# Selective-scan layers: a second buffer of turned x, one evacuation per projection, y summed in four column quarters, scatters spaced

## The chip, the core and the metric

The kernel runs on one NeuronCore of a Trainium2 chip. Its time is the device time of one execution in microseconds; where several runs are shown, the median is taken. The engines are TensorE (PE, with its weight loads as PEld), VectorE (DVE), ScalarE (ACT), GpSimd (POOL) and SyncE (SP, which issues most DMAs). Each engine takes its instructions in the order of the program, and engines wait for one another through semaphores.

## The reference, cut to what matters

An image batch of 4 x 64 x 64 positions with 96 channels passes through four layers. The first two are selective-scan layers, and the change lies in them alone. Cut to its core, one of them is:

```python
xz = x @ in_proj_w.T;  xc, z = split(xz)              # 192 channels each
xc = silu(depthwise_conv3x3(xc) + conv_b)
xs = stack([xc[order_k] for k in range(4)])           # four directions over the 4096 positions
x_dbl = einsum("bkdl,kcd->bkcl", xs, x_proj)          # dt (rank 6), B (16), C (16)
delta = softplus(dt_proj(dts) + dt_bias)
h = h * exp(delta * A) + (delta * u) * B              # step by step over 4096 positions
y = sum_n h[n] * C[n]                                 # 16 states
out = layernorm(merge of the 4 directions + D * xs) * silu(z) @ out_proj
```

In the first layer the four orders are two diagonal snakes and two radial orders, and the directions are merged with position-dependent weights. In the second they are rows, columns and both of them backwards, and they are added. A feed-forward part of layer 1 and the layers 2 and 3 (linear attention, a Fourier mixer, two small networks with fp8 products) follow. The change leaves them as they are.

## The kernel before

`scan_layers` works off eight batches: four images of the first layer (L0, `ordered`), then four of the second (L1). A batch has 4 directions (`kd`) x 4 segments of 1024 positions. A segment has 24 groups, each of 32 channels x 4 states on 128 partitions: 6 channel blocks (`cb`) x 4 state groups (`sg`). For a group

- ACT computes `da` = exp(dt * A) (`decay`, L1072), up to four groups ahead of the scan;
- DVE multiplies `t` = u * B (`enter`, L1076) and scans `h` = da * h + t (`recur`, L1083). DVE's order is fixed: two products, then the two scans;
- ACT keeps the last state (`keep`, L1094), POOL multiplies `hc` = h * C (`leave`, L1098);
- PE sums `hc` over the states into `y` in PSUM (`collect`, L1107).

At each of the six channel blocks PE first spreads `u` over 128 partitions (`spread_u`, L1065, "spread 0" to "spread 5" below): the product of groups 0, 4, 8, 12, 16 and 20 waits for it. When two blocks (8 groups) are summed, ACT copies `y` out (`yc`, L1136), PE turns it (L1148, "turn") and ACT writes it into `rows` (L1152). At the end of a segment `rows` goes to `y_tok` in DRAM: in L0's directions 0 and 1 as eight indirect scatters issued by POOL (L1162), else by SP.

While a segment is scanned, the next one is prepared (`prepare`). Its x is fetched position by position into `x_got`; PE turns it (`turn_x`, L897) and ACT copies it into `xs` (L908, L913); PE projects it in four parts (`project`, L934); ACT evacuates each part (`split`, L947 to L953); ACT forms the parts of softplus (`low`, L991 to L995, and `log`, L1006, between two table loads, since the rest of ACT needs another table); PE adds its four terms with identity matmuls (L1014, "sums") and ACT copies out `dt` (`keep_dt`, L1017); POOL multiplies `dtu` = dt * xs (L1023). `dt`, B and C go through DRAM to be spread over partitions. All of these use the one PSUM bank `m`, as does the turn of `y`. `xs` has one buffer, so the turning of the next x waits for the last `dtu` product of the segment before.

The order of the instructions in a batch is written by a planner, `Flow`: each operation has an estimated occupancy, a latency to other engines, a due time, and a mark `hard` for those that DVE waits for. It simulates the queues and emits the operations in that order. Where it sees PE idle it calls `keep_busy` (L1125), which issues matmuls with zero weights into the open sum, so that the PE clock stays up. Between batches a second planner, `Plan`, runs the merge of the batch that ended (`merge`) side by side with the convolution of the batch after the next (`front`); their tiles (`z_rows`, `xc`, `y_rows`, `yt`, `dx`, `halo`) lie in the pool `tmp` and are used only there. These stretches are called transitions below.

## Time and profile before

| | us |
|---|---|
| median of 3 runs (15260.49 to 15279.87) | 15266.5 |
| profiled execution, its own time | 15402.95 |
| its span | 15401.2 |
| start to the first product of the first batch | 386.2 |
| eight batches, first product to the end of the last scan: 1349.9, 1331.0, 1337.2, 1325.4 (L0), 1302.1, 1293.6, 1301.2, 1294.5 (L1) | 10534.9 |
| seven transitions between them: 211.9, 212.8, 225.4, 209.1, 159.7, 155.8, 98.7 | 1273.4 |
| after the last scan (last merge, layer 1's feed-forward, layers 2 and 3) | 3206.7 |

The four stretches are read from the first and last DVE instruction of each batch (lines 1076 and 1083) and add up to the span. Over the whole span PE is busy 90%, DVE 83%, POOL 60%, ACT 54%, the 16 DMA engines about a third; but PE's share holds the zero-weight matmuls, and the shares mix batches, transitions and the later layers. In a batch DVE has the most to do, and what is looked for is the time in which it stands still there.

### The profile page before, as it was taken

What the parts mean: (1) busy time and instruction counts of PE and PEld (TensorE: products, weight loads), DVE (VectorE), ACT (ScalarE), POOL (GpSimd) and SP (SyncE); (2) the same over time, 40 slices, a digit from 0 to 9 for tenths busy, and PEclk for the clock granted to TensorE, in tenths of its full rate; (3) what the DMA queues carried; (4) which work ended last, traced back from release to release, by engine and by line L of the source; (5) the groups of instructions that cost most, each with busy time, mean ns of one, the idle gap of its engine ahead of it and who ended that gap; (6) DMA issues with size and microseconds to landing.
All of it is one profiled execution on the core that took longest, in us unless ns stands there. A gap on an engine that the chain in (4) does not pass through costs nothing. (4 is left out here: it accounts for less than half of the span.)

```text
span 15401.2 us, 196660 instructions
## 1 busy us (share of the span) xinstructions
PE 13827.4 (90%) x74369; PEld 5096.1 (33%) x74369; DVE 12827.4 (83%) x9642; ACT 8327.7 (54%) x13421; POOL 9203.3 (60%) x4657
## 2 busy tenths in 40 slices
PE   8899899989998999899989998999899789998877
PEld 3233333333333333333333333333233244443344
DVE  1999799978997899799979997999899856555655
ACT  3666466646664666466656665666566423232333
POOL 0788678867886688667747774777577620000123
PEclk9999899989998999899989999999999999998888
DMA  2333433343334333433343334333433400000122
GB/s 67 117 113 125 150 111 111 126 148 112 111 127 146 106 118 128 148 116 117 123 152 124 118 124 152 126 118 120 156 119 120 142 10 11 19 15 12 52 72 71
DMA packets 662768, 1637.49 MB, mean 106 GB/s; under 512 B 102822, under 2 KB 268460, under 8 KB 658045
## 3 DMA queue, kind: packets, MB, share of 16 engines
q1 hardware_dynamic: 624956, 1549.37, 31.4%
q0 software_dynamic: 36864, 75.55, 1.7%
q8 instruction: 588, 9.63, 0.3%
q14 instruction: 360, 2.94, 0.1%
HBM read 1295.03 MB, written 329.58 MB: 105 GB/s over the span
## 5 line engine op out<-in xcount | busy, mean ns | idle before, releaser
L1098 POOL TENSOR_TENSOR hc<-h,bc 128x1024 f32<-128x1024 f32 x3072 | 7198.4, 2365 | 2216.1 <-DVE h L1083 1909.0
L1083 DVE TENSOR_TENSOR_SCAN h<-da,state,t 128x1024 f32<-128x1024 f32 x2304 | 5300.4, 2355 | 26.0 <-ACT state L1094 16.3
L1072 ACT ACTIVATE da<-dts,L_A_logs 128x1024 f32<-128x1024 f32 x3072 | 3520.0, 1151 | 1832.2 <-DVE h L1083 1786.7
L1076 DVE TENSOR_TENSOR t<-u,bc 128x1024 f32<-128x1024 f32 x3072 | 3629.8, 1239 | 267.6 <-PE u L1065 193.5
L1107 PE MATMUL y<-hc,gather_y 128*32 128x512 f32 x12288 | 3529.1, 620 | 311.9 <-POOL hc L1098 241.7
L1125 PE MATMUL y<-L_diag,zeros 96*32 96x256 f32 x7824 | 1986.3, 386 | 0.0
L1083 DVE TENSOR_TENSOR_SCAN h<-da,t 128x1024 f32<-128x1024 f32 x768 | 1717.4, 2287 | 17.3 <-ACT da L1072 9.1
L1065 PE MATMUL u<-dtu,spread 32*128 32x512 f32 x3072 | 1573.1, 632 | 120.0 <-DVE t L1076 109.2
L1125 PEld LDWEIGHTS y<-L_diag,zeros 96*32 96x32 f32 x7824 | 852.8, 111 | 1425.0 <-issue 926.1
L1107 PEld LDWEIGHTS y<-hc,gather_y 128*32 128x32 f32 x12288 | 595.8, 109 | 2021.1 <-issue 1029.1
L934 PE MATMUL m<-xs,proj 96*128 96x512 f32 (+1 forms) x2048 | 1070.2, 641 | 67.3 <-ACT spare L1152 32.5
L1642 DVE SCALAR_TENSOR_TENSOR hcv<-padv,taps,hcv 128x2048 f32<-128x2048 f32 x384 | 902.2, 2350 | 13.4
L1566 POOL MEMSET padp<- 128x2448 f32 x32 | 68.6, 2143 | 1400.8 <-PE d L1606 1378.3
L1023 POOL TENSOR_TENSOR dtu<-dt,xs 96x1024 f32<-96x1024 f32 x256 | 603.0, 2356 | 506.1 <-ACT dt L1017 501.1
L1606 PE MATMUL d<-padp,diag 32*32 32x512 f32 x25600 | 885.7, 601 | 2.0 <-ACT hcp L1621 2.0
L1065 PEld LDWEIGHTS u<-dtu,spread 32*128 32x128 f32 x3072 | 521.4, 188 | 943.6 <-issue 588.0
L1017 ACT COPY dt<-m 96x512 f32<-96x512 f32 x512 | 297.2, 580 | 694.5 <-PE m L1014 690.0
L1014 PE MATMUL m<-dtu,ident 96*96 96x512 f32 x1024 | 563.8, 632 | 72.7 <-ACT dt L1017 65.9
L1606 PEld LDWEIGHTS d<-padp,diag 32*32 32x32 f32 x25600 | 484.4, 103 | 369.8 <-issue 196.9
L934 PEld LDWEIGHTS m<-xs,proj 96*128 96x128 f32 (+1 forms) x2048 | 324.6, 181 | 770.6 <-issue 483.8
L947 ACT ACTIVATE sp_z<-m,L_dtb 96x512 f32<-96x512 f32 x512 | 350.0, 684 | 409.5 <-PE m L934 393.5
L1014 PE MATMUL m<-sp_log,ident 96*96 96x512 f32 x1024 | 539.2, 608 | 0.0
(275 smaller groups left out, 15495.8 us busy)
## 6 DMA issues: line engine op xcount, KB each, us to landing
bc<-bc_dram SPq DMA_DIRECT2D x1024, 512.0 KB
dts<-dt_dram SPq DMA_DIRECT2D x768, 512.0 KB
dt_dram<-dt SPq DMA_DIRECT2D x256, 384.0 KB
y_tok<-spare SPq DMA_DIRECT2D x64, 768.0 KB
dt<-y_tok SPq DMA_DIRECT2D x128, 384.0 KB
x_tok<-y_rows SPq DMA_DIRECT2D x32, 768.0 KB
z_t<-z_rows SPq DMA_DIRECT2D x64, 384.0 KB
dx<-x_tok SPq DMA_DIRECT2D x64, 384.0 KB
```

The source lines that it names most:

```text
L934: nc.tensor.matmul(v.ps, seg.proj[:, src, to], seg.xs[:, src, chunks[j]], start=src == 0, stop=src == 1)
L1014: nc.tensor.matmul(v.ps, k.ident[:C, :C], term[:, half, chunks[j]], start=at == 0, stop=at == 3)
L1023: nc.gpsimd.tensor_mul(seg.dtu[:, half], v.dt[:, half], seg.xs[:, half])
L1065: self.nc.tensor.matmul(seg.u[:, cols], self.spread[rows, :], seg.dtu[rows, half, cols], start=True, stop=True)
L1072: self.nc.scalar.activation(gr.da, gr.seg.dts[gr.cb], AF.Exp, scale=scale)
L1076: self.nc.vector.tensor_mul(gr.t, gr.seg.u, self.bc[:, 0, gr.sg, :])
L1083: self.nc.vector.tensor_tensor_scan(gr.h[:, order], gr.da[:, order], gr.t[:, order], start, op0=ALU.mult, op1=ALU.add)
L1098: self.nc.gpsimd.tensor_mul(gr.hc, gr.h, self.bc[:, 1, gr.sg, :])
L1107: nc.tensor.matmul(seg.y[at : at + GC, :], self.gather_y, gr.hc[:, part * CH : (part + 1) * CH], start=gr.sg == 0, stop=gr.sg == NSG - 1, ...
L1125: self.nc.tensor.matmul(gr.seg.y[at : at + GC, :256], self.zeros, gr.seg.bt.lay.diag.rearrange("p h t c -> p (h t c)")[:, :256], start=Fal ...
L1606: nc.tensor.matmul(pc[i][j * 32 : (j + 1) * 32, :], diag[mine, ON_PE.index(t), tap, :], pad[mine, j * 8 + dy : j * 8 + dy + 8, dx : dx + H ...
L1642: nc.vector.scalar_tensor_tensor(to, win, wt, to, op0=ALU.mult, op1=ALU.add)
```

## The change

1. **xs.** The tiles that only the transitions used become views of one tile `area` of 7 x 1024 values a partition, in the same number and size. Its last two sevenths (where `yt`, `dx` and `halo` lie) hold `xs` of the odd segments; the even ones keep their tile. The turning of x now waits for the `dtu` product of the segment before the last.
2. **Evacuation.** Each projected part leaves PSUM in one instruction (bias added, 128 rows with B and C, or 96). Abs and Relu follow from SBUF, as two more steps of `low` for each half. The projections no longer wait for the sums of the segment before; the first `low` step does.
3. **Sums of y.** `collect` issues four matmuls of 256 columns into four 32-column strips of the array in place of two of 512 into two. `turn` and `keep_rows` follow that layout (two copies in place of one), and so do the row order of `scan_idx` and the whole-segment stores (pieces of 384 values in place of 768).
4. **Scatters.** In the planner each scatter depends on the one before having landed.
5. **Planner.** `collect` counts 0.46 for 0.87; preparation is due 8 us later; a PE operation that waits for POOL is planned 1 us later; in front of hard operations `keep_busy` fills 0.35 of the gap for 0.7.

```diff
 class Op / Flow.run
+        self.lands = False
-                self.fill(start - free[engine])
+                self.fill(start - free[engine], 0.35 if op.hard else 0.7)
-                user.seen = max(user.seen, done if user.engine == engine else done + op.lat)
+                pad = 1.0 if (engine, user.engine) == ("POOL", "PE") else 0.0
+                near = user.engine == engine and not op.lands
+                user.seen = max(user.seen, done if near else done + op.lat + pad)
 Stream
+        self.area = k.t(w, [128, 7 * SEG], "area")
+    def shared(self, rings):
+        ...
+        cut("z_rows", 2, C, h=2, t=CH)
+        cut("xc", 3, 128, t=CH)
+        cut("y_rows", 1, 128, f=2, t=4, d=DI)
+        cut("yt", 1, C, h=2, t=CH)
+        cut("dx", 1, 128, t=CH // 128, d=DI)
+        cut("halo", 2, C, e=2, w=HW)
 prepare
-            x = Op(engine, occ, emit, deps, due=base + at, **kw)
+            x = Op(engine, occ, emit, deps, due=base + at + 8.0, **kw)
-                seg.xs = k.t(self.seg, [C, 2, SEG], "xs")
+                if seg.i % 2:
+                    seg.xs = self.area[:C, 5 * SEG :].rearrange("p (h t) -> p h t", h=2)
+                else:
+                    seg.xs = k.t(self.seg, [C, 2, SEG], "xs")
-                here += [b.get(("u", h)) for h in range(2)]
+                here += [before.before.o.get(("u", h)) for h in range(2)] if before and before.before else []
-            if what == 0:
-                nc.scalar.activation(v.z[:, half, cols], ps[:C], AF.Abs, bias=bias)
-            elif what == 1:
-                nc.scalar.activation(v.dt[:, half, cols], ps[:C], AF.Relu, bias=bias)
-            elif lay.bias_bc is None:
-                nc.scalar.copy(v.bc[:, cols], ps[C:])
+            if half == 0:
+                nc.scalar.activation(v.both[:, 0, cols], ps, AF.Identity, bias=lay.bias_bc[:, kd : kd + 1])
             else:
-                nc.scalar.activation(v.bc[:, cols], ps[C:], AF.Identity, bias=lay.bias_bc[C:, kd : kd + 1])
+                nc.scalar.activation(v.dt[:, 1, cols], ps, AF.Identity, bias=bias)
 low(half, what): Exp, 1 + z, 1 - r before; after:
+                nc.scalar.activation(z[:, half], dt[:, half], AF.Abs)
+                nc.scalar.activation(z[:, half], z[:, half], AF.Exp, scale=-1.0)
+                nc.scalar.activation(dt[:, half], dt[:, half], AF.Relu)
+                ...
 collect
-        for part in range(2):
-            at = (part * 2 + cb % 2) * GC
+        for part in range(4):
+            at = part * GC
             nc.tensor.matmul(
-                seg.y[at : at + GC, :],
+                seg.y[at : at + GC, cb % 2 * 256 : (cb % 2 + 1) * 256],
                 self.gather_y,
-                gr.hc[:, part * CH : (part + 1) * CH],
+                gr.hc[:, part * 256 : (part + 1) * 256],
 keep_busy
-        for _ in range(int((gap - 0.15) * 0.7 / 0.215)):
+        for _ in range(int((gap - 0.15) * share / 0.215)):
 turn, keep_rows
-        for j in range(CH // 128):
-            v = seg.ycs[pair][:, j::4] if fours else seg.ycs[pair][:, j * 128 : (j + 1) * 128]
-            nc.tensor.transpose(ps[:, j, :], v, k.ident)
+        for b in range(2):
+            mine = seg.ycs[pair][:, b * 256 : (b + 1) * 256]
+            for t in range(2):
+                nc.tensor.transpose(ps[:, b * 2 + t, :], mine[:, t::2] if twos else mine[:, t * 128 : (t + 1) * 128], k.ident)
-        self.nc.scalar.copy(seg.rows[:, :, :, pair * 64 : (pair + 1) * 64], ps)
+        for b in range(2):
+            at = pair * 64 + b * GC
+            self.nc.scalar.copy(seg.rows[:, :, :, at : at + GC], ps[:, b])
 store
-            return [Op("POOL", 1.25, partial(scatter, j), lat=4.0) for j in range(SEG // 128)]
+            for j in range(SEG // 128):
+                ops.append(Op("POOL", 1.25, partial(scatter, j), ops[-1:], lat=3.0))
+                ops[-1].lands = True
 batch
-                nxt.o["low", 0, 0].deps += [prev.o["spread", NCB - 1]] if prev else []
+                nxt.o["low", 0, 3].deps += [prev.o["spread", NCB - 1]] if prev else []
-                        0.87,
+                        0.46,
                         partial(self.collect, g2),
```

## The prediction

> **What bounds the kernel now.** I read the page's shares and slices first, then its groups of instructions, then the busy time of each engine in the four directions of one L0 and one L1 batch, and last the timelines of POOL, PE, ACT and DVE around the longest stop. From the page:
>
> ```profile
> PE 13827.4 (90%) x74369; PEld 5096.1 (33%) x74369; DVE 12827.4 (83%) x9642; ACT 8327.7 (54%) x13421; POOL 9203.3 (60%) x4657
> DVE  1999799978997899799979997999899856555655
> ...
> L1098 POOL TENSOR_TENSOR hc<-h,bc 128x1024 f32<-128x1024 f32 x3072 | 7198.4, 2365 | 2216.1 <-DVE h L1083 1909.0
> L1083 DVE TENSOR_TENSOR_SCAN h<-da,state,t 128x1024 f32<-128x1024 f32 x2304 | 5300.4, 2355 | 26.0 <-ACT state L1094 16.3
> L1076 DVE TENSOR_TENSOR t<-u,bc 128x1024 f32<-128x1024 f32 x3072 | 3629.8, 1239 | 267.6 <-PE u L1065 193.5
> ```
>
> DVE's digit is 9 in the batches and drops in the seven transitions. The last two lines show why the batches cannot lose much: DVE does 3072 products and 3072 scans and stands still for about 300 us in front of them, mostly for a spread `u`. The change leaves both instructions as they are, so those stops are all it can win in a batch. Where they are (four directions of L0's second batch, then of L1's second; columns: window, length, PE, PEld, DVE, ACT, POOL busy, PE clock, DMA share, GB/s):
>
> ```profile
> 1948.00:2287.20 339.20, 312.25 (x1034) 104.20 (x1034) 323.11 (x192) 219.25 (x465) 264.28 (x127) 0.95 0.34 111
> 2287.20:2625.60 338.40, 315.45 (x1035) 103.74 (x1036) 322.78 (x193) 213.98 (x380) 287.82 (x152) 0.95 0.35 117
> 2625.60:2955.20 329.60, 305.22 (x998) 96.69 (x994) 322.78 (x194) 210.81 (x306) 286.35 (x146) 0.97 0.38 122
> 2955.20:3279.00 323.80, 302.75 (x1011) 100.09 (x1010) 322.30 (x192) 207.54 (x345) 258.87 (x121) 0.97 0.33 111
> 8050.60:8378.00 327.40, 303.67 (x1022) 100.45 (x1020) 322.13 (x192) 214.78 (x310) 240.31 (x103) 0.98 0.36 117
> 8378.00:8700.90 322.90, 304.11 (x1036) 99.49 (x1036) 322.90 (x194) 211.05 (x305) 244.24 (x106) 0.99 0.39 124
> ```
>
> A direction of four segments takes DVE 322 us; L0's first two, those with scatters, take 16 us more, at a lower clock; L1 is at the floor. Eight batches at 4 x 322 would be 10304 us, and they take 10534.9: **231 us is the most the batches can give**. The DVE rows of the trace put 212 us of it in gaps over 0.3 us: 67.6 before the product that opens block 3 (spread 3), 60.6 at spread 4, 34.3 before the scan of group 12, 21.9 at spread 1, 6.1 at spread 2, 10.7 at spread 0, 1.6 at spread 5, 8.8 at the start of the first batch. One of them:
>
> ```profile
> 2313.53 1.00 POOL L1162 DMA_INDIRECT y_tok<-spare,scan_idx  x1 [1.31 <-DMA y_tok<-spare,scan_idx]
> 2317.64 0.97 POOL L1162 DMA_INDIRECT y_tok<-spare,scan_idx  x1 [3.10 <-issue]
> ...
> 2321.05 1.92 PE L1107 MATMUL y<-hc,gather_y 128*32 128x512 f32 x4 [2.56 <-POOL hc L1098]
> ...
> 2327.66 0.59 ACT L1136 COPY yc<-y 128x512 f32<-128x512 f32 x1 [5.84 <-PE y L1107]
> ...
> 2328.30 0.74 PE L1148 MATMUL m<-ident,yc 128*128 128x128 f32 x4 [0.69 <-ACT yc L1136]
> 2330.82 1.98 PE L1065 MATMUL u<-dtu,spread 32*128 32x512 f32 x4
> ...
> 2332.84 2.36 DVE L1076 TENSOR_TENSOR t<-u,bc 128x1024 f32<-128x1024 f32 x2 [5.81 <-PE u L1065]
> ```
>
> Two scatters in a row hold POOL; its product comes late, so the sum of y, its copy and its turn, and the spread queued behind that turn on PE.
>
> **Scatters.** In the built order of before POOL issues 60 pairs of scatters back to back and 40 single ones in L0's segments 1 to 5; after, each stands alone behind a pair of `hc`. A pair of `hc` takes 4.68 us, a scatter 1.01 with 0.16 ahead; a second one behind it waits 1.63 for the landing and takes 0.96. DVE makes a pair in 322/48 = 6.71 us. So 8.44 us (late by 1.7, more at each pair) becomes 5.85: POOL keeps pace, and each landing is covered by the next `hc` pair. Spread 3 follows from it: group 7's scan ends; `hc` 2.45 later; sum 1.05, copy 0.59, turn 0.74, spread 1.98: 6.8 us, against two pairs, 13.4, until its product. 6.6 spare covers one log with its table loads on ACT (1.28 + 2.00 + 1.28 = 4.56). The 67.6 us go. Bounds: nothing if POOL is late otherwise, 67.6 at most.
>
> **Second xs, single evacuation.** The second `xs` takes a wait for POOL off PE's turns of x, off the spreads and sums queued behind them, and off the fetches that SP issues once `x_got` is turned. The single evacuation: per segment four Abs at 0.684, four Relu at 0.679 and two copies of B and C at 0.63 (rows L947, L949, L951/L953), 6.7 us, become four at 0.68, 2.7; bank `m` is held 4.0 us less. Four more steps at 1.055 (L991 to L995) add 4.2 and three more row copies (2 x 0.375 by L566, for 0.579) 0.5: ACT +0.7 us a segment. ACT works 53 of 80.5 us there, so that is covered; uncovered it would be 128 x 0.7 = 93 us. In L0's directions 0 and 1 the log stands behind decay 13 or 14 in 28 of 32 segments, for 11 in 28 before. Then decay 14 is ready 1.15 + 1.06 + 4.56 + 1.15 = 7.9 us after scan 9, and its scan comes 15.7 after: scan 12's 34.3 go. The sums follow: 2.6 and spread 4's 1.98 end some 12 us after scan 9, against 20: of 60.6 I take 50, since in directions 2 and 3 sums still stand ahead of it. In the first segment of a batch spread 1 no longer stands behind a sum of y (in L1 also a projection), which waits for POOL's first product: 20 of 21.9, and 6 at spread 2. In most of L1 the log moves from decay 10 to decay 1 and the `dtu` products on POOL from groups 13 and 16 to 3 and 7, which only adds slack. In L0's directions 0 and 1 they move back to 15 and 19, each 2.36 us: POOL then needs 8.2 for a pair and is late by 1.5, a pair that the next ones, at 5.85, win back; the next segment's spreads 0 and 3 ask for them eight groups (27 us) and more later. SP's loads of `dts` follow the stores of `dt` as before, one of them two groups later; ACT waits for them 32 us in all now, and I leave that.
>
> **Sums of y.** The trace shows the two strips' matmuls starting 6 ns apart and the second passes 0.45 us later, so strips run side by side: 4 x 256 columns take half of 0.86 us. Bounds: eight 256-column passes at the fillers' 0.215 spacing, 1.7, if they ran in turn. At half, PE saves 24 x 0.43 = 10.3 us a segment, and 4842 fillers for 3912 give 3.1 back. PE is not what ends last, so this is only slack; at 1.7 PE would need 24 x 0.86 = 20.6 more a segment and be over-full.
>
> **What is late next.** In 8 of the 32 segments 15 of the 16 sums stand before spread 5, and the third `dt` copy, which frees the bank for the last of them, stands behind decay 21: 1.15 + 0.17 + 0.58 after scan 17, then three sums 2.57 and the spread 1.98: 6.45 of 6.71 us; in 4 more it is four sums behind the second copy, 7.3. With semaphores that is up to 1 us late, and 4.6 more at half clock. I charge 20 us for some 40 places of this kind, between 0 and 12 x 5.6 = 67.
>
> **Transitions.** The order there is the same on every engine but for one copy (0.17 each, 1.3 in all). `area` could add a wait of x on `yt`'s store at seven starts: 0, up to a DMA wait of 2.6 us each (18); I take 3. The stores in smaller pieces are read only by the merge, DMA engines being a third busy: 0, up to 1 us in each transition. Three more DVE instructions at the start lie within 386 us.
>
> The rows show half clock after short stops: PE's 0.95 in the first two windows is some 34 us at 0.5 in a direction, although no stop of PE there is longer than 2.9 us. [...] My sum charges nothing, because PE loses its longest stops with POOL's.
>
> **Sum.** 67.6 + 34.3 + 50 + 20 + 6 = 178 less 20, 1.3 and 3: 154 us. 15402.95 - 154 = 15249 in a profiled execution. That one stood 136.5 us above the median; taking 154 off the median gives **15112**. If all of the 136.5 lay in the gaps, only 154 x 94/231 = 63 would be won.
>
> **Rivals.** (1) Half of the gaps stay, or others take their place, because the log and the sums come as late as their due times (8 us later) allow: gain 30 to 110, about 15195. For it: gaps at spread 4 also stand in direction 2, where no scatter is. Against: the slack worked out above. (2) Nothing to measure, 15266: the spreads wait for another PE operation each time. For it: 56 of the 64 spreads 3 and 5 in L0's directions 0 and 1 stand directly behind a turn or sums (4 before); against: the turn's wait starts at POOL, which keeps pace. (3) Slower: with half of the fill in front of spreads the clock drops in every segment ahead of one. Price: a gap at spread 3 of 67.6/36 = 1.9 us in the 92 segments free of it now, +175, the rest unchanged: about 15440. Even with the 154 us won elsewhere it decides from some 81 such segments (154/1.9). Against: total fill rises by a quarter. (4) More: all 231 us go, and some waits in transitions: below 15066.
>
> **How the numbers follow.** Forecast (gain 110 to 200) 0.57; rival 1 0.18; rival 2 0.06; rival 3 0.13; rival 4 0.06. 0.2% (30 us) is about what a measurement can tell. Faster 0.57 + 0.18 + 0.06 = 0.81, same 0.06, slower 0.13. The range runs from all 231 us gone (15035) to 31 gone (15235); above it lie rivals 2 and 3, 0.19.
>
> **What would show it.** Right: directions 0 and 1 of L0 at 323 to 328 us and clock 0.98; scatter waits for their landing near nothing; DVE's wait for `u` in the batches under 60 us; L1 unchanged but for its first segments; four strips starting together, a sum's matmuls done in 0.6 us. Wrong: POOL behind at group 7 in spite of single scatters; new gaps at spread 5 or 1; half-clock stretches in L1; transitions longer by over 5 us each.

## The result, and the profile after

The changed kernel takes 15446.69 us (median of 4 runs, 15427.92 to 15489.57) where the kernel before takes 15263.49 (15244.15 to 15279.87): 1.0124 times as long, 95% interval 1.0100 to 1.0149. Forecast were 15112 and a range up to 15235.

The kernels below ran on several chips; the kernel before takes 15261 to 15264 us on some and 15374 to 15392 on others. So every time is given as a ratio to the kernel before on the same chip. Inside the batches the levels agree: 10534.9 us in the first profile of before (15402.95) and 10537.9 in a second one, `before_again` below (15252.45), so what is read there can be compared across chips. Spans are compared between `before_again` and the profile of the changed kernel.

The page of the changed kernel: shares of the span, the slices of the granted PE clock, and the costliest groups.

```profile
PE 13681.1 (89%) x88517; PEld 5605.3 (36%) x88517; DVE 12848.8 (83%) x9645; ACT 8276.4 (54%) x13549; POOL 9207.3 (60%) x4657
...
PEclk9898899888888888888888888888888899998888
...
L1117 DVE TENSOR_TENSOR_SCAN h<-da,state,t 128x1024 f32<-128x1024 f32 x2304 | 5270.2, 2328 | 5.4 <-ACT da L1106 3.7
L1110 DVE TENSOR_TENSOR t<-u,bc 128x1024 f32<-128x1024 f32 x3072 | 3596.1, 1216 | 472.4 <-PE u L1099 398.6
...
L1159 PE MATMUL y<-L_diag,zeros 96*32 96x256 f32 x9684 | 2610.3, 416 | 0.0
L1141 PE MATMUL y<-hc,gather_y 128*32 128x256 f32 x24576 | 2420.6, 441 | 48.5 <-POOL hc L1132 48.5
L1099 PE MATMUL u<-dtu,spread 32*128 32x512 f32 x3072 | 1734.6, 689 | 326.3 <-DVE t L1110 319.5
```

The same of `before_again`:

```profile
PEclk9999999999999999899999998999999899998888
...
L1107 PE MATMUL y<-hc,gather_y 128*32 128x512 f32 x12288 | 3533.3, 620 | 313.8 <-POOL hc L1098 243.4
L1125 PE MATMUL y<-L_diag,zeros 96*32 96x256 f32 x7824 | 1992.8, 387 | 0.0
...
L1065 PE MATMUL u<-dtu,spread 32*128 32x512 f32 x3072 | 1570.8, 631 | 117.2 <-DVE t L1076 107.1
```

DVE's products and scans take what they took. DVE waits 398.6 us for a spread `u` (193.5 in the first profile of before), and the clock digit is 8 in all but three slices of the batches, where it was 9 in all but three. The sums got shorter, and the time in zero-weight matmuls grew. The four directions of L1's second batch (window, length, PE, PEld, DVE, ACT, POOL busy, PE clock, DMA share, GB/s):

```profile
7971.70:8321.70 350.00, 315.72 (x1408) 117.50 (x1410) 323.29 (x193) 218.09 (x321) 240.66 (x103) 0.84 0.34 111
8321.70:8649.30 327.60, 299.28 (x1469) 113.67 (x1467) 322.52 (x192) 215.44 (x316) 243.59 (x105) 0.90 0.38 121
8649.30:8977.10 327.80, 299.65 (x1428) 112.62 (x1426) 322.41 (x193) 208.98 (x309) 243.34 (x105) 0.88 0.38 121
8977.10:9308.20 331.10, 299.97 (x1437) 113.88 (x1434) 322.83 (x193) 190.92 (x287) 243.57 (x105) 0.87 0.34 108
```

L1, at its floor of 322 before, is not any more. Between `before_again` and after the span grows by 175.4 us: batches 10537.9 to 10723.2 (+185.3; L1 alone +147), transitions 1113.6 to 1126.4 (+12.8), start -7.4, tail -15.5. DVE's gaps over 0.3 us in the batches go from 215 to 387 us: at spread 0 from 9.6 to 55.1, spread 1 22.8 to 39.6, spread 2 6.3 to 89.5, spread 5 1.2 to 96.3; only at spread 3 (76.2 to 30.8) and scan 12 (35.6 to 0) they shrink. Half clock (stretches with a granted clock of 0.5, counted to the batch in which they start): 529 us in the batches before, 2560 after.

Half clock and late spreads go together. Call a product that opens a block late when DVE stands still for more than 0.3 us in front of it, and the stretch ahead the 13.4 us before DVE was free for it, together with its wait. In the changed kernel's L1 batches 87 of 93 late products had half clock in the stretch ahead, 46% of it on the mean; of the 287 in time 218 had some, 19% on the mean.

How one L1 segment loses 1.0 us at spread 2. PE's and then DVE's timeline of the changed kernel (start, length, engine, line, operation; in brackets the wait before it):

```profile
8575.34 0.66 PE L1182 MATMUL m<-ident,yc 128*128 128x128 f32 x4 [1.19 <-ACT dt L1051]
8576.59 2.87 PE L1099 MATMUL u<-dtu,spread 32*128 32x512 f32 x4 [0.59 <-DVE t L1110]
8579.39 1.93 PE L1141 MATMUL y<-hc,gather_y 128*32 128x256 f32 x16
8581.25 2.02 PE L1048 MATMUL m<-dtu,ident 96*96 96x512 f32 x2
8583.07 1.91 PE L1048 MATMUL m<-sp_z,ident 96*96 96x512 f32 x2
8584.77 1.92 PE L1048 MATMUL m<-dt,ident 96*96 96x512 f32 x2
8586.48 1.65 PE L1048 MATMUL m<-sp_log,ident 96*96 96x512 f32 x2
8588.06 0.64 PE L1141 MATMUL y<-hc,gather_y 128*32 128x256 f32 x8
8588.51 0.60 PE L1159 MATMUL y<-L_diag,zeros 96*32 96x256 f32 x2
8589.04 1.10 PE L1048 MATMUL m<-dtu,ident 96*96 96x512 f32 x2
...
8593.38 1.98 PE L1099 MATMUL u<-dtu,spread 32*128 32x512 f32 x4
...
8595.40 2.37 DVE L1110 TENSOR_TENSOR t<-u,bc 128x1024 f32<-128x1024 f32 x2 [1.00 <-PE u L1099]
```

PE stands still for 1.19 and 0.59 us; then its clock is halved (0.5 granted from 8577.49 for 10.24 us): the spread takes 2.87 for 1.98, each of the four 512-column matmuls behind the sum (two passes each) 1.6 to 1.8 to the next start, against 0.93 at full clock in the last of them shown. From 8576.59 to the next spread PE has no pause, and that spread is late by 1.0. In this stretch PE ends last, although DVE is the engine with the higher share of a batch.

### The profile page after: what moved, and what is told of

Read it like the earlier page. It is cut to its first block, busy times and chain, and to the rows that moved or that the text cites. A ratio compares the mean times of both kernels' runs of the same rounds, so it can differ in the third digit from the quotient of the medians.

```text
span 15426.1 us, 225496 instructions
## 1 busy us (share of the span) xinstructions
PE 13681.1 (89%) x88517; PEld 5605.3 (36%) x88517; DVE 12848.8 (83%) x9645; ACT 8276.4 (54%) x13549; POOL 9207.3 (60%) x4657
## 3 DMA queue, kind: packets, MB, share of 16 engines
q14 instruction: 361, 2.96, 0.1%
## 5 line engine op out<-in xcount | busy, mean ns | idle before, releaser
L1110 DVE TENSOR_TENSOR t<-u,bc 128x1024 f32<-128x1024 f32 x3072 | 3596.1, 1216 | 472.4 <-PE u L1099 398.6
L1159 PE MATMUL y<-L_diag,zeros 96*32 96x256 f32 x9684 | 2610.3, 416 | 0.0
L1141 PE MATMUL y<-hc,gather_y 128*32 128x256 f32 x24576 | 2420.6, 441 | 48.5 <-POOL hc L1132 48.5
L1099 PE MATMUL u<-dtu,spread 32*128 32x512 f32 x3072 | 1734.6, 689 | 326.3 <-DVE t L1110 319.5
L1117 DVE TENSOR_TENSOR_SCAN h<-da,t 128x1024 f32<-128x1024 f32 x768 | 1710.6, 2268 | 12.4 <-ACT da L1106 12.4
L1159 PEld LDWEIGHTS y<-L_diag,zeros 96*32 96x32 f32 x9684 | 1112.3, 120 | 1391.4 <-issue 634.5
L1141 PEld LDWEIGHTS y<-hc,gather_y 128*32 128x32 f32 x24576 | 755.9, 118 | 1761.5 <-issue 1295.7
L1682 DVE SCALAR_TENSOR_TENSOR hcv<-padv,taps,hcv 128x2048 f32<-128x2048 f32 x384 | 902.2, 2350 | 13.4
L964 PE MATMUL m<-area,proj 96*128 96x512 f32 (+1 forms) x1024 | 602.2, 707 | 28.7 <-ACT dt L977 20.5
L1182 PE MATMUL m<-ident,yc 128*128 128x128 f32 x1536 | 303.7, 326 | 361.0 <-ACT dt L979 116.1
L964 PE MATMUL m<-xs,proj 96*128 96x512 f32 (+1 forms) x1024 | 592.5, 699 | 34.5 <-ACT dt L979 15.0
L1057 POOL TENSOR_TENSOR dtu<-dt,xs 96x1024 f32<-96x1024 f32 x128 | 302.0, 2360 | 520.2 <-ACT dt L1051 473.7
L1048 PE MATMUL m<-sp_z,ident 96*96 96x512 f32 x1024 | 585.8, 656 | 0.0
```

The costliest lines, as they stand in the source:

```text
L964: nc.tensor.matmul(v.ps, seg.proj[:, src, to], seg.xs[:, src, chunks[j]], start=src == 0, stop=src == 1)
L1048: nc.tensor.matmul(v.ps, k.ident[:C, :C], term[:, half, chunks[j]], start=at == 0, stop=at == 3)
L1099: self.nc.tensor.matmul(seg.u[:, cols], self.spread[rows, :], seg.dtu[rows, half, cols], start=True, stop=True)
L1110: self.nc.vector.tensor_mul(gr.t, gr.seg.u, self.bc[:, 0, gr.sg, :])
L1117: self.nc.vector.tensor_tensor_scan(gr.h[:, order], gr.da[:, order], gr.t[:, order], start, op0=ALU.mult, op1=ALU.add)
L1141: nc.tensor.matmul(seg.y[at : at + GC, cb % 2 * 256 : (cb % 2 + 1) * 256], self.gather_y, gr.hc[:, part * 256 : (part + 1) * 256], start=g ...
```

## The experiments

Unless a diff says otherwise, a kernel is the one named, and nothing else differs.

**1. The extra 1 us in the plan.** In the changed kernel 262 of 384 turns stand directly in front of a spread (8 before), and the planned delay of POOL's results was the first suspect.

`after_no_pad`:

```diff
-                pad = 1.0 if (engine, user.engine) == ("POOL", "PE") else 0.0
+                pad = 0.0
```

> The changed kernel with one planner entry undone: an operation on PE that waits for POOL is again planned without the extra 1 us. In the built order the turn of y then never stands directly in front of a spread (262 of 384 turns in the changed kernel do), and 951 zero-weight matmuls stand directly in front of spreads (none in the changed kernel). Theory P (the extra 1 us puts sums and turns directly in front of the spreads, PE stands still there with nothing to fill it, and its clock halves): the four L1 batches go back from 1330-1336 to 1295-1305 us each, half-clock time in the batches from 2560 to under 900 us, total 15110 to 15260. Theory Q (four short matmuls side by side leave PE too little to do, so that the clock falls whatever the order is): L1 batches stay at 1325 or more, total 15400 or more. Theory E (the evacuation in one instruction and the later steps of low hold PE up): also 15400 or more.

`before_pad`, on the kernel before:

```diff
-                user.seen = max(user.seen, done if user.engine == engine else done + op.lat)
+                user.seen = max(user.seen, done if user.engine == engine else done + op.lat + (1.0 if (engine, user.engine) == ("POOL", "PE") else 0.0))
```

> The kernel before with that one planner entry alone: an operation on PE that waits for POOL is planned 1 us later. In the built order 130 of 384 turns then stand directly in front of a spread (8 before) and no zero-weight matmul stands directly in front of one (1004 before). Theory P: slower than the kernel before by 80 to 200 us, L1 batches 1315 to 1340 us, with half-clock stretches of 150 to 400 us in each (24 to 65 before). Theories Q and E, and the theory that the order of these operations does not matter: 15264 within 30 us.

Measured: 1.0103 (1.0086 to 1.0119) and 1.0008 (0.9997 to 1.0019). Theory P falls twice; both times are as theories Q and E expected. With the extra 1 us alone, half clock in L1's batches rises to 167 to 201 us each, yet they take 1294 to 1297 us, the floor, and 232 of the 367 products in time had half clock in the stretch ahead: half clock by itself need not cost anything. L0 does not show the same: with 147 to 184 us of half clock a batch its four batches take 27 us more than in `before_again`, and how much of that is the clock is not shown.

**2. The quarters.** `after_halves` takes them off the changed kernel, `before_quarters` puts them alone on the kernel before; both with layout, row copies, store pieces and planned length. The core:

```diff
-        for part in range(2):
-            at = (part * 2 + cb % 2) * GC
+        for part in range(4):
+            at = part * GC
...
-                        0.87,
+                        0.46,
                         partial(self.collect, g2),
```

> The changed kernel with the sums of y again as two matmuls of 512 columns into two strips, their layout, row copies and planned length as before; all else, the extra 1 us too, stays. 170 of 384 turns stand directly in front of a spread. Theory Q: back to 15270 or below, half clock in L1 batches under 100 us each. Theory P: still 15380 to 15480, half clock in L1 batches 250 us or more each. If both are needed together: in between, 15300 to 15380.

> The kernel before with the sums of y in four column quarters alone (four matmuls of 256 columns, layout, row copies, store pieces and planned length 0.46 with it). 12 of 384 turns stand directly in front of a spread, and 2227 zero-weight matmuls do. Theory Q: slower by 100 us or more, L1 batches 1315 us or more. Theory P: 15264 within 40 us, L1 batches 1293 to 1303 us, half clock in them under 100 us each.

Measured: 1.0032 (1.0020 to 1.0044), between theories P and Q, and 1.0224 (1.0207 to 1.0241), more than the whole change and what Q expected (L1 batches of 1354 to 1360 us). But Q's reason, a PE with too little to do, is not what the trace shows (below). The quarters are the largest part of the loss, and the rest that stays in `after_halves` wins nothing either. PE and DVE of `before_quarters` around a spread 3 in L1:

```profile
8463.89 1.10 PE L1014 MATMUL m<-sp_log,ident 96*96 96x512 f32 x2
8466.18 0.75 PE L1148 MATMUL m<-ident,yc 128*128 128x128 f32 x4 [1.19 <-ACT dt L1017]
8466.86 0.64 PE L1107 MATMUL y<-hc,gather_y 128*32 128x256 f32 x8
8467.31 1.89 PE L1125 MATMUL y<-L_diag,zeros 96*32 96x256 f32 x8
8469.14 1.98 PE L1065 MATMUL u<-dtu,spread 32*128 32x512 f32 x4
...
8471.15 2.36 DVE L1076 TENSOR_TENSOR t<-u,bc 128x1024 f32<-128x1024 f32 x2 [2.96 <-PE u L1065]
```

The turn waits for the bank, and behind it four zero-weight matmuls take 1.89 us of a time that is no longer free; 2.96 us are lost. The four appear as x8: each of these f32 matmuls is two records (passes) in the trace, so one of 256 columns takes 0.43 us, where `keep_busy` counts 0.215. It plans to fill 0.7 of a gap and fills 1.4 of it. The page shows it too: in `before_quarters` the sums' group falls from 12288 passes of 512 columns (3533 us busy in `before_again`) to 24576 of 256 (2329), and the zero-weight group rises from 7824 passes (1993 us) to 12998 (3394). More is put in than was saved.

```profile
L1125 PE MATMUL y<-L_diag,zeros 96*32 96x256 f32 x12998 | 3393.7, 405 | 0.0
L1107 PE MATMUL y<-hc,gather_y 128*32 128x256 f32 x24576 | 2329.4, 408 | 431.4 <-POOL hc L1098 415.6
```

The fill is not the whole of it. In L1's batches 208.5 of the 245.2 us by which products came late stand behind half clock in the stretch ahead (93 of 149 late products; 27 of the 231 in time), but none of the 45 late ones at spread 4 has any.

**3. Fill, order or the matmuls themselves?** Four kernels. `before_quarters_old_plan` has quarters in the old order:

```diff
-                        0.46,
+                        0.87,
                         partial(self.collect, g2),
...
-        kept = flow.add("ACT", 0.7, partial(self.keep_rows, seg, pair), [t], due=at + 18.0, bank=-1)
+        kept = flow.add("ACT", 0.5, partial(self.keep_rows, seg, pair), [t], due=at + 18.0, bank=-1)
```

> The kernel before with the four column quarters, but planned at the old 0.87 a sum: every instruction of PE stands where it stood before, 4186 zero-weight matmuls in the built order among them; only each sum is four matmuls of 256 columns, 0.46 us in place of 0.88 by the traces. Theory H (the short side-by-side matmuls themselves cost time or clock): 1.010 times the kernel before or more. Theory O (the order that follows from a planned 0.46) and theory F (the zero-weight matmuls that the planner adds into the time it believes free, 6773 for 4186): 0.997 to 1.003 times the kernel before.

`after_plan_087`, the changed kernel with the same number back:

```diff
-                        0.46,
+                        0.87,
                         partial(self.collect, g2),
```

> The changed kernel with one number back: a sum of y is planned at 0.87 for 0.46 and stays four short matmuls. 3126 zero-weight matmuls in the built order (5116 in the changed kernel), none directly in front of a spread, 122 turns directly in front of one (262). Theories O and F: 1.004 times the kernel before or less, L1 batches 1295 to 1312 us. Theory H: 1.010 or more, as the changed kernel (1.0124).

`after_fill_035`:

```diff
-                self.fill(start - free[engine], 0.35 if op.hard else 0.7)
+                self.fill(start - free[engine], 0.35)
```

> The changed kernel with half of its zero-weight matmuls: 2289 for 5116 in the built order, otherwise the same order but for nothing. Theory F (they take the PE time that the quarters freed, so that what is late stays late): 1.007 times the kernel before or less, PE's clock lower than the changed kernel's 0.87. Theory C (the falling clock is what costs): slower than the changed kernel, 1.016 or more, with more half-clock time than its 2560 us in the batches. Theory O: within 0.3% of the changed kernel's 1.0124.

`before_quarters_fill_035`, on `before_quarters`:

```diff
-        for _ in range(int((gap - 0.15) * 0.7 / 0.215)):
+        for _ in range(int((gap - 0.15) * 0.35 / 0.215)):
```

> The kernel before with quarters planned at 0.46, in the same order as that experiment (1.0224), with half of the zero-weight matmuls: 3144 for 6773 in the built order. Theory F: 1.006 times the kernel before or less, the gaps at spreads 2 and 3 (303 us there) under 120. Theory O: 1.015 or more. Theory C: 1.025 or more, with more half-clock time than the 2705 us there.

Measured, in this order: 1.0065 (1.0040 to 1.0090), 1.0107 (1.0076 to 1.0137), 1.0094 (1.0066 to 1.0123), 1.0253 (1.0224 to 1.0282). No single theory survives. In the old order the quarters cost 0.65%: the expectation of O and F is missed, that of H too. `after_plan_087` comes out as H expected, `after_fill_035` as O did, `before_quarters_fill_035` as O and C did; F is missed every time. The order and the fill that follow from a planned 0.46 cost more than the quarters in the old order, 1.0224 against 1.0065. Half of the fill hardly matters: in the changed kernel half clock in the batches rises from 2560 to 3976 us and DVE's gaps fall from 387 to 313, with a ratio whose interval overlaps the changed kernel's; on `before_quarters` half clock rises from 1345 to 3635 and the gaps from 525 to 575. A fuller PE and a slower PE are two ways to the same late spread.

**4. What PE saves, put back.** `before_quarters_refilled` and `quarters_refilled_once`: quarters in the old order, and behind each sum that does not close a pair of blocks two zero-weight matmuls, or one (1.1 in place of 2.1 in the added line).

```diff
         self.open = gr if gr.sg < NSG - 1 else None
+        self.keep_busy(0.15 + 2.1 * 0.215 / 0.7)
```

> The four quarters in the old order (that experiment took 1.0065 times the kernel before), with two zero-weight matmuls of 256 columns behind every sum that does not close a pair of blocks: 8794 for 4186 in the built order, so PE is about as long at work as in the kernel before. Theory C (the time that the short sums free on PE is time in which its clock falls, and spreads and sums pay for it): 0.998 to 1.003 times the kernel before, half clock in each L1 batch back from 273-300 us to under 120. Theory L (the layout costs: two row copies on ACT for one, stores in smaller pieces, four matmuls to issue for two): 1.004 or more, whatever the clock does.

> The four quarters in the old order with one zero-weight matmul of 256 columns (0.43 us) behind every sum that does not close a pair of blocks, which is what the sum got shorter by (0.882 to 0.456): work on PE as in the kernel before. Theory C (only the clock makes the quarters cost in the old order): 0.997 to 1.003 times the kernel before, half clock in L1 batches under 110 us each (273-300 without refill, 24-65 in the kernel before). Theory L (row copies and store pieces cost): 1.005 or more.

Measured: 1.0176 (1.0159 to 1.0193) with two, 1.0047 (1.0030 to 1.0064) with one. L1's second batch in `before_again`, `before_quarters_old_plan`, with one and with two (columns as above):

```profile
7879.60:9173.00 1293.40, 1206.83 (x4102) 397.25 (x4100) 1288.36 (x768) 840.39 (x1215) 970.66 (x415) 0.99 0.37 119
```

```profile
8074.10:9386.80 1312.70, 1174.10 (x5630) 427.92 (x5628) 1290.20 (x768) 836.73 (x1262) 970.30 (x415) 0.90 0.37 117
```

```profile
7956.70:9269.60 1312.90, 1211.37 (x6204) 474.70 (x6203) 1289.64 (x768) 840.46 (x1262) 970.33 (x415) 0.96 0.37 117
```

```profile
8035.10:9371.10 1336.00, 1284.16 (x6778) 526.61 (x6776) 1292.26 (x768) 838.53 (x1262) 972.59 (x415) 0.99 0.36 115
```

The first row is the floor. Without refill PE is busy 33 us less and the clock falls to 0.90: 273 us of half clock, 19 us lost. With two matmuls the clock is back at 0.99, PE is busy 77 us more, and 43 us are lost, mostly in the gaps at spreads 3 and 5 (127 and 152 us in the whole run, 76 and 1 in `before_again`). One matmul restores PE's work (1211) but not the clock, 0.96 with 96 to 109 us of half clock in L1 and 143 to 198 in L0 (89 to 106 before); in the batch shown it loses 19.5 us, as much as none. In L1, 58 of the 59 late products without refill and 38 of the 42 with one matmul had half clock in the stretch ahead (of those in time 166 of 321 and 34 of 338), but only 4 of the 134 with two. So there both are PE being late, once by its clock and once by its work. The 1.0047 is between theories C and L; in L0, where 57 of the 93 late products with one matmul had half clock ahead, how much of it is clock and how much row copies and stores is not settled.

**5. The other parts alone.** `before_spaced`, on the kernel before:

```diff
-            return [Op("POOL", 1.25, partial(scatter, j), lat=4.0) for j in range(SEG // 128)]
+            ops = []
+            for j in range(SEG // 128):
+                ops.append(Op("POOL", 1.25, partial(scatter, j), ops[-1:], lat=3.0))
+                ops[-1].lands = True
+            return ops
```

> The kernel before with the scatters spaced alone (each planned behind the landing of the one before it). The prediction's step: the 67.6 us of gaps at spread 3 of L0's directions 0 and 1 fall under 25, the four L0 batches get shorter by 40 to 70 us in all: 0.995 to 0.998 times the kernel before. Rival (the sums and turns are late there for another reason, or the gaps move to spreads 4 and 5): 0.998 to 1.002, with the same sum of gaps in L0 (178 us) within 25.

`before_evac`, the change's part 2 on the kernel before, its core:

```diff
-                nc.scalar.activation(v.z[:, half, cols], ps[:C], AF.Abs, bias=bias)
-                nc.scalar.activation(v.dt[:, half, cols], ps[:C], AF.Relu, bias=bias)
+                nc.scalar.activation(v.dt[:, 1, cols], ps, AF.Identity, bias=bias)
...
+                nc.scalar.activation(z[:, half], dt[:, half], AF.Abs)
+                nc.scalar.activation(dt[:, half], dt[:, half], AF.Relu)
```

> The kernel before with the single evacuation of each projected part alone (Abs and Relu as two more steps from SBUF, the log behind them, projections free of the sums of the segment before). The prediction's step: the gaps at spread 4 and at the scan of group 12 (60.6 and 34.3 us) shrink by half or more: 0.994 to 0.998 times the kernel before. Rival (the log and the sums come later and the gaps move to spread 5, as in the changed kernel where spread 5 has 96 us): 0.999 to 1.005, gaps at spread 5 over 40 us (1.6 before).

`rest_only`, the changed kernel less quarters, extra 1 us and halved fill:

```diff
-                self.fill(start - free[engine], 0.35 if op.hard else 0.7)
+                self.fill(start - free[engine])
-                pad = 1.0 if (engine, user.engine) == ("POOL", "PE") else 0.0
+                pad = 0.0
-        for part in range(4):
+        for part in range(2):
-                        0.46,
+                        0.87,
```

> The changed kernel without the quarters, with sums planned at 0.87, without the extra 1 us behind POOL and without the halved fill: the second xs, the single evacuation, the spaced scatters and the later due times remain. If these are worth what the prediction gave them (some 150 us in its sum, none of it from the quarters): 0.988 to 0.994 times the kernel before. If they cancel one another, or their gain was never there: 0.998 to 1.004.

Measured: 0.9912 (0.9895 to 0.9928), 0.9979 (0.9969 to 0.9988), 1.0011 (1.0001 to 1.0020). **Spaced scatters alone win 0.9%**, 15135.61 us for 15262.14: more than the step gave them. `before_evac` ends in the range of its step, but not by its mechanism: the gaps at spread 4 grow (54.6 us in `before_again`, 86.7 here), and what it wins is at spread 3 (76.2 to 33.1) and scan 12 (35.6 to 19.9). `rest_only` is where its second expectation had it: the parts cancel one another, or some of the gain was never there. What held a scatter of the kernel before (`before_again`) back, in us and times:

```profile
L1162 POOL DMA_INDIRECT y_tok<-spare,scan_idx x256: 958/1003/1192, 497.5 to 5678.0; - x128
...
  DMA y_tok<-spare,scan_idx: 107.7, 52
  DVE t L1076: 27.9, 18
  issue: 24.5, 141
```

and in `before_spaced`:

```profile
L1162 POOL DMA_INDIRECT y_tok<-spare,scan_idx x256: 998/1007/1192, 497.7 to 5571.0; - x128
...
  issue: 30.6, 187
  PE m L1148: 1.1, 7
  DVE h L1083: 0.3, 2
```

The 108 us of waiting for a landing are gone. DVE's gaps in the batches fall from 215 to 127 us, at spread 3 from 76.2 to 22.4, but also at spread 4 from 54.6 to 17.3 and at scan 12 from 35.6 to 17.6, places that the sum had given to xs and the evacuation. L0's batches get 113 us shorter in all, L1's 21 us longer. L0's second batch, `before_again` and then `before_spaced`, directions 0 and 1:

```profile
1908.50:2254.40 345.90, 316.51 (x1026) 104.84 (x1027) 323.27 (x192) 219.06 (x465) 264.04 (x127) 0.94 0.33 108
2254.40:2597.90 343.50, 317.21 (x1044) 104.28 (x1042) 323.10 (x193) 214.63 (x381) 288.87 (x153) 0.96 0.36 116
```

```profile
1879.70:2209.80 330.10, 312.33 (x1054) 106.10 (x1054) 322.57 (x193) 219.10 (x465) 264.65 (x127) 0.96 0.35 113
2209.80:2540.80 331.00, 315.38 (x1060) 105.33 (x1058) 322.40 (x194) 215.21 (x381) 291.62 (x153) 0.97 0.37 122
```

**6. Who gives it back?** With xs, evacuation and later due times the 0.9912 becomes 1.0011. One at a time on `before_spaced`; `spaced_evac` and `spaced_xs` add the change's parts 2 and 1:

```diff
+                if seg.i % 2:
+                    seg.xs = self.area[:C, 5 * SEG :].rearrange("p (h t) -> p h t", h=2)
...
-                here += [b.get(("u", h)) for h in range(2)]
+                here += [before.before.o.get(("u", h)) for h in range(2)] if before and before.before else []
```

> The kernel before with spaced scatters (0.9912 alone) and the second xs buffer. Theory X (the second xs lets projections and sums move to places where spreads stand behind them): 0.997 or more, gaps at spreads 1 and 5 over 60 us together (33 with the scatters alone). Otherwise 0.988 to 0.993; the prediction gave the second xs 26 us in first segments, 0.9895.

> The kernel before with spaced scatters and the single evacuation. If the parts add up (0.9912 and 0.9979 alone): 0.987 to 0.991, the fastest of all so far. Theory Y (the gain of the evacuation is the same lateness that the scatters caused): 0.990 to 0.994. If the two disturb each other: 0.996 or more.

`spaced_due`:

```diff
-            x = Op(engine, occ, emit, deps, due=base + at, **kw)
+            x = Op(engine, occ, emit, deps, due=base + at + 8.0, **kw)
```

> The kernel before with spaced scatters and preparation due 8 us later. Theory D (with later due times the sums of the next segment gather in front of spreads 4 and 5, 4 of them before spread 4 and 15 before spread 5): 0.997 or more, gaps at spreads 4 and 5 over 80 us (19 with the scatters alone). Otherwise 0.989 to 0.993.

Measured: 0.9984 (0.9974 to 0.9995), 0.9939 (0.9923 to 0.9956), 1.0024 (1.0014 to 1.0033). On top of the scatters the second xs and the due times lose 0.7% and 1.1%. The evacuation's 0.3% is not clear of noise: its interval overlaps that of `before_spaced`, and the profiled spans are alike (15158.2 and 15160.2 us). The three do not add up (together they lose 1.0%); one order of PE replaces another. The due times are the clearest: of a segment's 16 sums, 11.3 (L0) and 11.1 (L1) then stand between spread 4 and spread 5 in the built order, for 7.2 and 6.0. PE in such a stretch of `spaced_due` in L0, and DVE behind it:

```profile
2629.21 3.52 PE L1109 MATMUL y<-hc,gather_y 128*32 128x512 f32 x8
2632.66 1.14 PE L1016 MATMUL m<-sp_z,ident 96*96 96x512 f32 x2
2633.64 1.02 PE L1016 MATMUL m<-dt,ident 96*96 96x512 f32 x2
2634.49 1.02 PE L1016 MATMUL m<-sp_log,ident 96*96 96x512 f32 x2
2635.45 1.05 PE L1109 MATMUL y<-hc,gather_y 128*32 128x512 f32 x4
...
2643.76 1.98 PE L1067 MATMUL u<-dtu,spread 32*128 32x512 f32 x4
...
2645.78 2.37 DVE L1078 TENSOR_TENSOR t<-u,bc 128x1024 f32<-128x1024 f32 x2 [2.61 <-PE u L1067]
```

Two pairs of groups take DVE 13.4 us, and PE has more than that to do between the spreads, 16.5 us without a pause. The first two sums of y run at half clock (3.45 us to the next start, where one takes 0.98 later); without that, by these spacings, some 15.0 us would be left, an estimate and still too much. In L1 none of the 31 late products at spread 5 has half clock in the stretch ahead. So theory D holds: the gaps at spread 5 go from 1.9 to 114.7 us. Theory X holds in size but not in place: with the second xs the gaps are at spread 4 (17 to 107 us). For the evacuation theory Y holds, at the edge of its range: its own gain (0.21% without the spacing) was in the gaps that the spacing closes, and afterwards only what it moves is left (spread 4, 17.3 to 61.7 us).

PE's work between two spreads can be estimated from the built order and the full-clock spacings of the trace (0.47 us a 512-column pass of a sum, 0.88 or 0.46 a sum of y, 0.43 a zero-weight matmul, 1.92 a spread). Ahead of spread 5, mean of L0 and of L1, beside the gaps at spread 5:

| kernel | PE work, us (DVE: 13.4) | gaps at spread 5, us |
|---|---|---|
| `before_again` | 12.8, 12.8 | 1.2 |
| `before_quarters_old_plan` | 11.0, 10.7 | 31.7 |
| `quarters_refilled_once` | 12.4, 12.4 | 20.0 |
| `before_quarters_refilled` | 13.8, 14.1 | 151.6 |
| `spaced_due` | 15.5, 15.8 | 114.7 |
| after | 13.5, 10.6 | 96.3 |

By this estimate the kernel before has 0.6 us to spare. Half clock comes on top: 270 to 365 us of it a batch in the changed kernel, 273 to 341 in `before_quarters_old_plan`, where PE has little to do ahead of spread 5 and is late there all the same, almost all of it in L1 (29.0 of the 31.7 us).

**7. The base, and the halved fill where it acts.** `before_again` is the kernel before, with no line changed.

> The kernel before, unchanged. If this execution is near 15264: the seven transitions sum to about 1130 us (1273 in the first profile; the kernels profiled since near that level have 172 to 183 us in each of the first four) and the batches to 10520-10545, that is, the 137 us lay in the transitions and the batches' gaps were there to win in full. If the batches are 137 us shorter and the transitions as before, the gaps of the first profile were partly its own.

`spaced_fill_035`, on `before_spaced`:

```diff
-                self.fill(start - free[engine])
+                self.fill(start - free[engine], 0.35 if op.hard else 0.7)
...
-        for _ in range(int((gap - 0.15) * 0.7 / 0.215)):
+        for _ in range(int((gap - 0.15) * share / 0.215)):
```

> The kernel before with spaced scatters and the changed kernel's halved fill in front of hard operations: 3808 zero-weight matmuls in the built order for 4326, 518 directly in front of spreads for 1036. Rival 3 of the prediction (half of the fill in front of spreads lets the clock drop in every segment): 0.997 times the kernel before or more, half clock in L1 batches over 150 us each (48-78 with the scatters alone). Otherwise 0.988 to 0.993; below 0.990 it is the fastest, because the zero-weight matmuls, two passes of 0.215 us each, stand in front of spreads that are late.

`before_again` took 15252.45 us in one execution, with transitions of 1113.6 us (1273.4 in the first profile), batches of 10537.9 (10534.9) and DVE gaps of 215 (212). So the 137 us lay in the transitions, and the gaps were there to win in full. `spaced_fill_035` takes 0.9953 (0.9939 to 0.9968), 0.4% more than `before_spaced`, with 72 to 109 us of half clock in L1's batches (48 to 79): between its two expectations. `before_spaced` stays the fastest kernel of the study and beats both given ones.

## Why the prediction was wrong

- **"PE is not what ends last, so this is only slack."** This step failed. The windows that stood under the bound already had PE busy 302.75 to 315.45 of 323.80 to 339.20 us in L0; I read DVE's digit and did not weigh that row. PE was the second bound, by the estimate above 0.6 us from the first in a stretch between spreads, and its time is not free in either direction. With less work the clock fell (0.90 for 0.99 in L1's second batch; 0.65% in all in the old order, in L1 nearly always behind half clock), and the planner puts zero-weight matmuls at twice their counted length where it believes time to be free (1.76% with two put back in the old order, with the clock up; with the planner's own order and fill 2.24%, part of it behind half clock). The sizes of the sum were right: a quarter sum takes 0.456 us to the next operation, half of 0.882.
- **The clock: nothing charged, "because PE loses its longest stops with POOL's".** This failed too. The scatters' waits for a landing went (0.5 us left), and half clock rose from 529 to 2560 us: it came behind short stops as well (last section).
- **Scatters: 67.6.** Right in mechanism, mis-sized: alone they win 127 us of the median, L0's batches getting 113 shorter in the profiles and L1's 21 longer. The gap at spread 3 fell by 54; another 55 us fell at spread 4 and scan 12.
- **Second xs, single evacuation: 34.3 + 50 + 20 + 6 = 110.** Wrong. Alone the evacuation won 0.21%, and not at spread 4; on top of the scatters it wins nothing (0.27% slower, not clear of noise) and the second xs loses 0.72%. The slack worked out for one chain (log, sums, spread) was used by what PE had moved into it.
- **What is late next: 20, between 0 and 67.** The place was right, the size was not: the gaps at spread 5 grew by 95 us. Later due times alone bring 113. My working used 2.57 and 1.98 us for the last operations ahead of a spread and did not add up the whole stretch against 13.4.
- **Transitions: 4.3.** 12.8 measured, inside the bounds.
- **Rival 3, 15440.** Its total was right to 7 us and its consequence, half clock in every segment, was seen, but not its cause. In the changed kernel's built order no zero-weight matmul stands directly in front of a spread, so 0.35 has nothing to halve: with 0.7 in both places the order of every engine is the same. Where the halved fill does act (`spaced_fill_035`) it costs 0.4%. So the near hit of its total is luck. Nor does its price hold: 167 to 201 us of half clock in an L1 batch cost nothing in `before_pad`.
- **Rival 1's reason** (gaps come back because the due times allow it) is what `spaced_due` shows; I took it for a smaller gain where it was a loss.

Open: how the 1.24% divides between order, fill and clock cannot be read from single edits, since they do not add up; and `after_halves` (1.0032) still holds the extra 1 us and the later due times together.

## What to carry to other kernels

An engine that is 93% busy in the window that matters is a second bound even when another one sets the pace: add up its work between two of its deadlines and compare with what the pacing engine needs there, for every stretch, before calling anything slack. Filler work that is issued in order is work: count its real length (here 0.43 us a matmul where 0.215 was planned), and expect it to eat what an optimisation frees. And test the parts of a compound change one by one: here one part of five wins 0.9%, and the others together hide it.

## What the runs showed of the hardware

- In these runs the PE clock was halved without a long stop. In L1's second batch of `before_quarters_old_plan` PE's longest stop after the first segment is 2.10 us, and 26 of the batch's 29 half-clock stretches start there; in the 3.4 us ahead of these, the length of the shortest stretch, PE was busy for 0.32 to 0.86 of the time (median over all 29: 0.53). The stretches of that batch last 3.4, 6.8, 10.2 or 13.7 us.
- In the same batch of the changed kernel the median is 0.50 over 41 stretches. After its first segment PE's longest stop is 3.23 us, and ahead of the 38 stretches there PE was busy for 0.29 to 0.81 of 3.4 us; but a window at full clock with PE busy for 0.48 had full clock behind it as well. So these shares give no limit.
- What half clock cost did not follow from its length: in L1, 167 to 201 us a batch for nothing in `before_pad`, 273 to 300 us a batch for 16 us on the mean in `before_quarters_old_plan`, where 58 of 59 late products had it in the 13.4 us ahead or in their wait.
